# Attention scores of other groups' keys by seven products, with VectorE's order in phase 1 set by a virtual clock and convolution multiplications on GpSimd

## The chip, the cores and the metric

The kernel runs on one core of a Trainium2 chip, everything in float32. The metric is device microseconds (us) for one execution; before the change the median of three runs is 2495.1 us (2494.08 to 2495.87).

## What is computed

The input x is 4 x 2048 tokens of 512 numbers. Two blocks follow each other, each with a layer norm in front, a layer norm behind and a residual sum:

```
def _L0_attn_ref(x, Wq, bq, Wk, bk, Wv, bv, Wo, bo):
    q = relu(x @ Wq + bq); k = relu(x @ Wk + bk); v = relu(x @ Wv + bv)
    e = einsum('bqd,bkd->bqk', q, k) / sqrt(D)
    e = e - NEG * causal
    e = exp(e - max(e)); attn = e / sum(e)
    return relu(einsum('bqk,bkd->bqd', attn, v) @ Wo + bo)

def _gated_bottleneck(x2d, conv_w, conv_b, gamma, beta, lin_w, lin_b):
    xc = einsum('ngf,gf->ng', x2d.reshape(n, g, 4), conv_w) + conv_b
    xn = (xc - mean) * rsqrt(var + BN_EPS) * gamma + beta   # mean, var over all tokens
    return gelu(xn) @ lin_w.T + lin_b

x = x + _layernorm(_L0_attn_ref(_layernorm(x), ...))
x = x + _layernorm(_L0_ffn_ref(_layernorm(x), ...))   # two branches gated by the top 32 of a softmax
```

The batch norm's mean and variance run over all 8192 tokens. So a phase 1 (attention, and the features xc of both branches) has to end before phase 2 (softmax, top 32, products with the weight) can begin. For scores that could not be masked by -10000 alone there is a second path with every key; it isn't executed with these inputs.

## The kernel before

**Tiling.** Phase 1 goes through 16 groups of 512 tokens, four of each batch (`n.g` is 0 to 3 in the batch). A group attends to its own keys, under the causal mask, and to those of the batch's earlier groups. So its scores have `n.nk` = 4 (g+1) tiles of 128 keys by 512 queries. They are kept transposed (keys on partitions) in the pool `stp` of 16 tiles.

**Seven products.** Projections with Wv, Wq, Wk and Wo (`Seven`, L390 on) are Strassen products in Winograd's form: halves of 256 in each of the three dimensions, seven products in place of eight. One product is `times` (L403): 4 matmuls of 128x128 weights by 256 columns. p1, p6, p7 and p4 add up in one PSUM accumulator, which is read out between them (`put`, L426): VectorE adds the copied sums b, c5 and c53 (products 2, 5 and 5+3, copied by ScalarE, L423) to the accumulator, so each of these products waits for the sum before it. The right operands are sums of quarters of the tokens (`token_sums`, L366), the left ones sums of weights that are made once, stored to HBM and fetched for each group through a `Ring` of 14 tiles of 256 KB (L267 on). For Wo the left operand is made of the values (`value_sums`, L376).

**One step** (`steps`, L687 on) works on group n and prepares the next one, nxt. PE's order is written down by hand (`manual_schedule(engines={PE})`, L846):

1. `scores` (L489): for each tile of keys 4 matmuls (L499), a copy by ScalarE (L508), mask (L511) and maximum (L518) on VectorE. `between` puts the group's seven products with Wo (object O), the next group's transposed tokens and their sums in between.
2. V of nxt, the fold of the maxima (L527, L529), Q of nxt, `spread` of the maxima by a matmul (L542), K of nxt.
3. `weights` (L544): subtraction on VectorE (L550), exponential on ScalarE (L551), sums on GpSimd (L555).
4. `attend` (L567) for four tiles of 128 queries, then `attended` (L581) evicts it, `residual` (L585 on) does two layer norms with the reciprocal square root on GpSimd (L137) and the residual sum x1 on GpSimd (L593), and `convolve` multiplies with both branches' weights (L613) and reduces by four (L614), all on VectorE. Then come DMAs of x1, xn2, its transpose and the transposed features.

The tile scheduler orders VectorE, ScalarE, GpSimd and SP's queue in these steps: by priority, among what is ready by its own model of time. All loads and stores named above go through SP's queue in one order.

**The end of phase 1.** In the last step the products of `bound` (L652, four pieces, `filler`) stand in for the missing projections: one after the scores, one after the fold, two after the first features of the last group. `prepare` (L661 on) readies the branches in groups 1 and 2: its second half, from L670 on, transposes the linear weights and makes three rows of bfloat16 parts with a single buffer (`prep`), each sent off by a DMA before the next is made.

Of the kernel before, what the change touches and what calls it, by code (L numbers as in the profile page):

```python
# [26 lines left out]
F32 = mybir.dt.float32  # L28
# [24 lines left out]
def sandwich_kernel(ctx: ExitStack, tc: tile.TileContext, io: dict, out: bass.AP):  # L53
# [75 lines left out]

    xn2_d = [dram.tile([GT, D], F32, name=f"xn2_{i}") for i in range(NGRP)]  # L130
# [65 lines left out]
    def phase1(every_key):  # L196
# [5 lines left out]
        kp = enter("kp", GB)  # L202
# [3 lines left out]
        ap = enter("ap", 3)  # L206
# [10 lines left out]
        def load(b, g, joint=True):  # L217

            n = Group()
            n.b, n.g, n.i = b, g, b * GB + g  # L220
            n.x = []
            n.rstd = sm.tile([P, TPG], F32, name="rstd_x")
            var = sm.tile([P, TPG], F32, name="var_x")
            n.mv = sm.tile([P, TPG, nc.vector.BN_AGGR_DIM], F32, name="mv_x")
            for t in range(TPG):
                xt = xp.tile([P, D], F32, name="xt")
                row = n.i * GT + t * P
                nc.sync.dma_start(xt, xf[row : row + P, :])
                st = sm.tile([P, nc.vector.BN_STATS_DIM], F32, name="st_x")
                nc.vector.bn_stats(st, xt)  # L230
                nc.vector.bn_aggr(n.mv[:, t, :], st)
                n.x.append(xt)
                if not joint:
                    nc.vector.tensor_scalar_add(var[:, t : t + 1], n.mv[:, t, 1:2], LN_EPS)
                    inv_sqrt(n.rstd[:, t : t + 1], var[:, t : t + 1])
            if joint:
                nc.vector.tensor_scalar_add(var, n.mv[:, :, 1], LN_EPS)
                inv_sqrt(n.rstd, var)
            return n
# [12 lines left out]
        def turn_x(n):  # L252

            for t in range(TPG):
# [5 lines left out]
                nc.sync.dma_start(xnT_d[n.i][t * P : (t + 1) * P, :], n.x[t])  # L260

# [5 lines left out]
        class Ring:  # L267
# [6 lines left out]
            def fill(self):  # L274
                while len(self.made) < len(self.order):
# [4 lines left out]
                    t = wring.tile([P, D], F32, name="wb")  # L280
                    w = io[f"L0_attn_W{m}"]
# [84 lines left out]
        def token_sums(n):  # L366
# [3 lines left out]
            nc.vector.tensor_tensor(T1, B12, B11, ALU.subtract)  # L370
            nc.vector.tensor_tensor(T2, B22, T1, ALU.subtract)
            nc.vector.tensor_tensor(B12, B22, B12, ALU.subtract)
            nc.gpsimd.tensor_tensor(T4, B21, T2, ALU.subtract)
            n.right = {1: B11, 2: B21, 3: B22, 4: T4, 5: T1, 6: T2, 7: B12}

        def value_sums(n, most):  # L376
# [3 lines left out]
            if most:  # L380
                S1, S2 = (one.tile([P, 2, H], F32, name=f"T{k}") for k in (1, 2))
                nc.vector.tensor_tensor(S1, A21, A22, ALU.add)
                nc.vector.tensor_tensor(S2, S1, A11, ALU.subtract)
                nc.vector.tensor_tensor(A21, A11, A21, ALU.subtract)
                n.left = {1: A11, 2: A12, 4: A22, 5: S1, 6: S2, 7: A21}
            else:
                n.left[3] = one.tile([P, 2, H], F32, name="T4")
                nc.vector.tensor_tensor(n.left[3], A12, n.left[6], ALU.subtract)

        class Seven:  # L390


            def __init__(self, n, m):
                self.n, self.m, self.bias = n, m, biases.get(m)
                self.room = None
                if m == "o":
# [6 lines left out]
            def times(self, ps, k, new):  # L403

                i, w = self.w[(AS_RIGHT if self.m == "o" else AS_LEFT)[k]]
                w = w.rearrange("p (c d) -> p c d", c=2)
                left, right = (self.n.left[k], w) if self.m == "o" else (w, self.n.right[k])
# [10 lines left out]
                ring.drop(i)  # L418

            def copied(self, ps, pool_tag):  # L420
                t = self.room.pop() if self.room else two.tile([P, D], F32, name=pool_tag)
# [4 lines left out]
            def put(self, r, s, other=None):  # L426

                at = self.dst[:, 2 * r : 2 * r + 2, s * H : (s + 1) * H]
                acc = self.acc.rearrange("p (d t) -> p d t", d=2)
                with tc.high_priority():  # L430
                    if other is not None:
                        nc.vector.tensor_tensor(at, acc, other.rearrange("p (d t) -> p d t", d=2), ALU.add)  # L432
# [27 lines left out]
            def p6(self):  # L460
                self.times(self.acc, 6, False)
                self.put(0, 1, self.c53)

            def p7(self):
                self.times(self.acc, 7, False)
                self.put(1, 1, self.c5)

            def p4(self):
                self.times(self.acc, 4, False)
# [19 lines left out]
        def scores(n, kTs, between=None):  # L489

            n.nk = GB * TPG if every_key else (n.g + 1) * TPG
            n.st = []
            n.mx = one.tile([P, GT], F32, name="mxsum")
            for kt in range(n.nk):
                off = first(n, kt)
                ps = ps_mm.tile([P, GT], F32, name="mm")
                k = kt % TPG * P
                for c in range(NC):
                    nc.tensor.matmul(  # L499
                        ps[:, off:],  # L500
                        lhsT=kTs[kt // TPG][:, c, k : k + P],
                        rhs=n.qT[:, c, off:],
                        start=(c == 0),
                        stop=(c == NC - 1),
                    )
                st = stp.tile([P, GT], F32, name="st")
                own = kt - n.g * TPG
                nc.scalar.copy(st[:, off:], ps[:, off:])  # L508
                if 0 <= own < TPG:
                    q = slice(own * P, (own + 1) * P)  # L510
                    nc.vector.tensor_tensor(st[:, q], st[:, q], causal, ALU.add)  # L511
                if every_key and own > 0:
                    q = slice(0, min(own, TPG) * P)
                    nc.vector.tensor_scalar_add(st[:, q], st[:, q], neg_raw)
                if kt == 0:
                    nc.vector.tensor_copy(n.mx, st)
                else:
                    nc.vector.tensor_tensor(n.mx[:, off:], n.mx[:, off:], st[:, off:], ALU.max)  # L518
                n.st.append(st)
                if between:  # L520
                    between(kt)

        def fold(src, op):

            tp = ps_tp.tile([P, NC, P], F32, name="tp")
            for t in range(TPG):
                nc.tensor.transpose(tp[:, t, :], src[:, t * P : (t + 1) * P], ident)  # L527
            r = sm.tile([P, TPG], F32, name="fold")
# [3 lines left out]
        def maxima(n):  # L532

            m = fold(n.mx, ALU.max)
# [9 lines left out]
        def weights(n):  # L544

            n.sum = one.tile([P, GT], F32, name="mxsum")
            for kt in range(n.nk):
# [6 lines left out]
                else:  # L554
                    nc.gpsimd.tensor_tensor(n.sum[:, off:], n.sum[:, off:], w, ALU.add)  # L555

        def sums(n):
            s = fold(n.sum, ALU.add)
            n.rsum = sm.tile([P, TPG], F32, name="rsum")
            nc.vector.reciprocal(n.rsum, s)  # L560
# [15 lines left out]
        def attended(n, t, acc):  # L576


            a = (ap if n.nk == GB * TPG else stp).tile([P, D], F32, name="a" if n.nk == GB * TPG else "st")
# [3 lines left out]
            return a  # L583

        def residual(n, t, a):  # L585

            ti = n.i * TPG + t
            xr = two.tile([P, D], F32, name="xr")
            nc.sync.dma_start(xr, xf[ti * P : (ti + 1) * P, :])
            m, r = row_norm(sm, a, "a")  # L590
            nc.vector.tensor_scalar(a, a, m, r, ALU.subtract, ALU.mult)
# [3 lines left out]
            store = nc.scalar if n.i == NGRP - 1 else nc.sync  # L595
            store.dma_start(x1_d[n.i][t * P : (t + 1) * P, :], x1)
            m, r = row_norm(sm, x1, "x1")
            xn2 = ap.tile([P, D], F32, name="a")
# [546 lines left out]
```

## Time and profile before

| | us |
|---|---|
| median of three runs | 2495.1 |
| the profiled execution | 2491.96 |
| its span, first to last instruction | 2490.1 |
| first group's preparation (from the start) | about 130 |
| steps of groups 1 to 15, up to the last scores | 130 to 1715 |
| end of phase 1 | 1715 to 1790.3 |
| phase 2 | 1790.3 to 2490.1 |
| a batch's four steps (933.92, 1001.38, 1096.15, 1219.09 to 1368.79) | 67.5, 94.8, 122.9, 149.7 |

The page lists busy times by engine: PE (TensorE's matmuls), PEld (its weight loads, beside them), DVE (VectorE), ACT (ScalarE), POOL (GpSimd), and SP, whose queue issues DMAs. A float32 matmul appears as two instructions. Matmuls overlap, so the duration of one (592 ns for 512 columns) is longer than the distance to the next. A row of a group reads: line, engine, operation, what it writes and reads, shapes, count, busy us, mean ns of one, idle time of the engine before it and what ended that.

The costliest groups of phase 1 by busy time are the attention products L567 (424.5 us up to 1716), the scores L499 (481.6) and the seven products L410 (790.1, the sum of its rows). The granted clock is 1.00 through the steps.

### The profile page before, as it was taken

What the parts mean: (1) busy time and instruction counts of PE and PEld (TensorE: products, weight loads), DVE (VectorE), ACT (ScalarE), POOL (GpSimd) and SP (SyncE); (2) the same over time, 40 slices, a digit from 0 to 9 for tenths busy, and PEclk for the clock granted to TensorE, in tenths of its full rate; (3) what the DMA queues carried; (4) which work ended last, traced back from release to release, by engine and by line L of the source; (5) the groups of instructions that cost most, each with busy time, mean ns of one, the idle gap of its engine ahead of it and who ended that gap; (6) DMA issues with size and microseconds to landing.
All of it is one profiled execution on the core that took longest, in us unless ns stands there. A gap on an engine that the chain in (4) does not pass through costs nothing.

```text
span 2490.1 us, 27105 instructions
## 1 busy us (share of the span) xinstructions
PE 2434.8 (98%) x7778; PEld 1401.1 (56%) x7778; DVE 1715.0 (69%) x3707; ACT 1020.5 (41%) x2208; POOL 969.2 (39%) x913
## 2 busy tenths in 40 slices
PE   8999999999999999999999999999999999999997
PEld 3775756587675658767565876754333333333332
DVE  3677564567655456765645676453699999999997
ACT  2332313232231323223131332312278787878785
POOL 1122210311221031122103122212288888898986
PEclk9999999999999999999999999999999999999998
DMA  6565543466554246655434665320434444444441
GB/s 214 183 170 170 155 124 100 112 184 169 173 153 126 96 114 184 169 175 151 127 98 112 185 170 161 108 89 3 128 76 106 110 111 118 108 119 105 118 104 53
DMA packets 551902, 325.96 MB, mean 131 GB/s; under 512 B 388672, under 2 KB 443456, under 8 KB 551744
## 3 DMA queue, kind: packets, MB, share of 16 engines
q1 hardware_dynamic: 548208, 320.97, 46.3%
q10 hardware_dynamic: 3024, 2.11, 0.3%
q8 instruction: 65, 1.06, 0.2%
q0 software_dynamic: 512, 1.06, 0.1%
q14 instruction: 93, 0.76, 0.1%
HBM read 231.22 MB, written 92.80 MB: 130 GB/s over the span
## 4 chain that ended last, share of the span: by engine, by line
PE 58%; POOL 4%; ACT 4%; DVE 3%; issue 3%; DMA 1%; SPq 0%; POOLq 0%; ACTq 0%; DVEq 0%
PE mm L499 13%; PE mm L971 12%; PE acc L567 11%; PE acc L410 9%; PE mm L410 7%; PE lg L929 3%; PE tp L1038 1%; PE lg L932 1%; POOL e_si L959 1%; POOL xs L965 1%; POOL h L1078 1%; ACT L909 1%; DVE st L550 1%; POOL mxsum L555 1%; DMA xt<-in_L_attn_x_dram 1%
## 5 line engine op out<-in xcount | busy, mean ns | idle before, releaser
L499 PE MATMUL mm<-qT,kT 128*128 128x512 f32 (+3 forms) x1280 | 481.6, 529 | 0.4 <-ACT st L508 0.4
L567 PE MATMUL acc<-vo,st 128*128 128x512 f32 x1088 | 474.7, 592 | 1.4 <-ACT st L551 1.4
L499 PEld LDWEIGHTS mm<-qT,kT 128*128 128x128 f32 x1280 | 235.2, 190 | 216.5 <-issue 193.5
L567 PEld LDWEIGHTS acc<-vo,st 128*128 128x128 f32 x1088 | 205.4, 190 | 241.5 <-issue 235.2
L971 PE MATMUL mm<-w_L_ffn_weight,xnT 128*128 128x512 f32 x512 | 248.9, 609 | 0.6 <-ACT xc_si L632 0.6
L508 ACT COPY st<-mm 128x512 f32<-128x512 f32 (+3 forms) x160 | 83.2, 520 | 401.1 <-PE mm L499 400.7
L971 PE MATMUL mm<-w_L_ffn_weight,xsT 128*128 128x512 f32 x512 | 239.9, 612 | 2.6 <-ACT xsT L1044 2.6
L553 POOL COPY mxsum<-st 128x512 f32<-128x512 f32 x16 | 9.7, 609 | 543.6 <-ACT st L551 463.4
L137 POOL TENSOR_TENSOR rs_a<-ve_a,neg_half 128x1 f32<-128x1 f32 x64 | 35.4, 554 | 362.6 <-DVE ve_a L146 358.8
L518 DVE TENSOR_TENSOR mxsum<-mxsum,st 128x512 f32<-128x512 f32 (+2 forms) x144 | 95.7, 664 | 116.3 <-ACT st L508 113.9
L410 PE MATMUL acc<-T,wb 128*128 128x256 f32 x720 | 170.7, 380 | 2.8 <-DVE qT L432 2.8
L555 POOL TENSOR_TENSOR mxsum<-mxsum,st 128x512 f32<-128x512 f32 (+2 forms) x144 | 167.7, 1165 | 13.7 <-ACT st L551 2.9
L410 PE MATMUL mm<-xnT,wb 128*128 128x256 f32 x720 | 170.1, 379 | 0.0
L410 PE MATMUL acc<-xnT,wb 128*128 128x256 f32 x720 | 165.2, 379 | 0.0
L971 PEld LDWEIGHTS mm<-w_L_ffn_weight,xsT 128*128 128x128 f32 x512 | 93.1, 192 | 111.1 <-issue 94.2
L410 PEld LDWEIGHTS acc<-T,wb 128*128 128x128 f32 x720 | 135.9, 190 | 30.4 <-issue 6.5
L971 PEld LDWEIGHTS mm<-w_L_ffn_weight,xnT 128*128 128x128 f32 x512 | 92.3, 190 | 106.6 <-issue 105.5
L410 PEld LDWEIGHTS acc<-xnT,wb 128*128 128x128 f32 x720 | 136.8, 190 | 25.0 <-issue 4.5
L410 PEld LDWEIGHTS mm<-xnT,wb 128*128 128x128 f32 x720 | 135.0, 190 | 23.8 <-issue 7.2
L582 ACT ACTIVATE st<-st 128x512 f32<-128x512 f32 x48 | 30.2, 630 | 246.7 <-DVE st L581 246.7
L937 DVE MAX8 m_si<-rest_si 128x8 f32<-128x512 f32 x192 | 131.1, 683 | 0.0
L945 DVE MATCH_REPLACE8 rest_so<-m_so,rest_so 128x512 f32<-128x512 f32 x192 | 129.7, 675 | 0.0
(223 smaller groups left out, 4285.5 us busy)
## 6 DMA issues: line engine op xcount, KB each, us to landing
x<-x SPq DMA_DIRECT2D x124, 256.0 KB, 2.9
xt<-in_L_attn_x_dram SPq DMA_DIRECT2D x64, 256.0 KB, 4.5
xr<-in_L_attn_x_dram SPq DMA_DIRECT2D x64, 256.0 KB, 2.9
xn<-xn SPq DMA_DIRECT2D x64, 256.0 KB, 2.9
out_dram<-h SPq DMA_DIRECT2D x64, 256.0 KB, 2.0
wb<-Z_v SPq DMA_DIRECT2D x60, 256.0 KB, 2.8
wb<-Z_q SPq DMA_DIRECT2D x60, 256.0 KB, 3.4
wb<-Z_k SPq DMA_DIRECT2D x60, 256.0 KB, 2.6
```

Of the source, the lines that this page charges most:

```text
L137: nc.gpsimd.tensor_tensor(dst, src, neg_half[:, : src.shape[1]], ALU.pow)
L410: nc.tensor.matmul(ps[:, d * H : (d + 1) * H], lhsT=left[:, c, d * P : (d + 1) * P], rhs=right[:, c, :], start=(new and c + d == 0), stop= ...
L499: nc.tensor.matmul(ps[:, off:], lhsT=kTs[kt // TPG][:, c, k : k + P], rhs=n.qT[:, c, off:], start=(c == 0), stop=(c == NC - 1),)
L508: nc.scalar.copy(st[:, off:], ps[:, off:])
L518: nc.vector.tensor_tensor(n.mx[:, off:], n.mx[:, off:], st[:, off:], ALU.max)
L555: nc.gpsimd.tensor_tensor(n.sum[:, off:], n.sum[:, off:], w, ALU.add)
L567: nc.tensor.matmul(acc, lhsT=n.st[kt][:, t * P : (t + 1) * P], rhs=vos[kt // TPG][:, kt % TPG, :], start=(kt == 0), stop=(kt == nk - 1),)
L582: nc.scalar.activation(a, a, AF.Relu)
L929: nc.tensor.matmul(n.lg[br], lhsT=xa[n.k][br][:, n.t * P : (n.t + 1) * P], rhs=lin_T[br], start=True, stop=False)
L937: nc.vector.max(n.m8[br], n.rest[br] if k else n.lg[br])
L945: nc.vector.match_replace(n.rest[br], n.m8[br], n.rest[br], -LOWEST)
L971: nc.tensor.matmul(ps, lhsT=lhsT[:, c, :], rhs=wf[:, c, :], start=(c == 0), stop=(c == NC - 1))
```

## The change

- Scores of other groups' keys become `Seven` objects, named by the number of the keys' group. Their left operands are the keys' quarters and sums (`key_sums`, new), stored to HBM as seven tiles per group and fetched through the ring; the right ones are sums of the queries (`query_sums`, `last_query_sum`, new). The result is four `st` tiles. The sums out of PSUM are made in two pieces of 128x256, and the maxima are taken tile by tile (`maximum`). The pool of keys shrinks to one buffer.
- Scores of the group's own keys stay tile by tile (`score_tile`).
- VectorE joins PE in the order by hand. A class `Pace` keeps a virtual time of PE (advanced by `pace.pe` at each matmul group) and one of VectorE; VectorE's work comes as jobs of three ranks, generators that yield their duration and a pause. `run` emits the next piece of the first job that is ready by this clock; `flush` emits the rest of a job at once.
- `residual` and `convolve` become one generator, `chain`, of lowest rank, with at most two open at once, carried over into the next step. Its two multiplications are GpSimd's, but in the last group.
- The second half of `prepare` comes before the attention products, and in the last step three pieces of `bound` come before `spread` and one behind the features.

```
 class Pace:
+    def add(self, rank, pieces, after=0.3):
+        job = [self.t + after, pieces]
+        self.ranks[rank].append(job)
+        return job
+    def step(self, job):
+        try:
+            us, pause = next(job[1])
+            self.v = max(self.v, job[0]) + us
+            job[0] = self.v + pause
+        except StopIteration:
+            ...
+    def open(self):
+        return [*self.ranks[0], *self.ranks[1], *self.ranks[2][:2]]
+    def run(self):
+        while self.v < self.t:
+            ready = [j for j in self.open() if j[0] <= self.v]
+            if ready:
+                self.step(ready[0])
+            else:
+                self.v = min([self.t] + [j[0] for j in self.open()])
+    def pe(self, us):
+        self.t += us
+        self.run()
```

```
+        def key_sums(n):
+            A11, A21, A12, A22 = quarters(n.kT)
+            S1, S2, S4 = (one.tile([P, 2, H], F32, name=f"Q{k}") for k in (1, 2, 4))
+            nc.vector.tensor_tensor(S1, A21, A22, ALU.add)
+            ...
+            nc.vector.tensor_tensor(S4, A12, S2, ALU.subtract)
+            for k, t in ((2, A12), (5, S1), (1, A11), (3, S4), (6, S2), (7, A21), (4, A22)):
+                nc.sync.dma_start(keys_d[n.i, k].rearrange("p (c d) -> p c d", c=2), t)
+            yield 0.9, 0.0
```

The products, now with `pace.pe(1.72)` behind each, and their sums:

```
             def put(self, r, s, other=None):
+                scores = isinstance(self.m, int)
+                if other is not None:
+                    self.job = pace.add(0, work(0.8 if scores else 0.7, self.written, r, s, other))
+                else:
+                    self.written(r, s)
+                if scores and r != s:
+                    after = 0.3 if other is not None else 1.2
+                    self.n.maxima += [pace.add(1, work(0.66, self.maximum, st), after) for st in self.dst[2 * r : 2 * r + 2]]
...
             def p6(self):
+                pace.flush(self.job)
                 self.times(self.acc, 6, False)
                 self.put(0, 1, self.c53)
```

The step:

```
+                for t in range(TPG):
+                    score_tile(n, n.g * TPG + t, n.kT)
+                    pace.pe(0.86 * (TPG - t))
+                    for step in of_O[t]:
+                        step()
+                        ...
+                if n.g:
+                    pace.add(0, work(0.9, last_query_sum, n))
+                    A = Seven(n, n.b * GB)
+                    A.p2(), A.p5(), O.p7(), A.p1(), A.p3(), O.p4(), A.p6()
+                    for i in range(1, n.g):
+                        N = Seven(n, n.b * GB + i)
+                        N.p2(), N.p5(), A.p7(), N.p1(), N.p3(), A.p4(), N.p6()
+                        A = N
...
                     V = Seven(nxt, "v")
-                    V.p2(), V.p5()
+                    V.p2()
+                    pace.flush(tokens)
+                    if n.g:
+                        A.p7()
+                    V.p5()
+                    if n.g:
+                        A.p4()
```

The chain of a tile of queries:

```
+            m, r = row_norm(sm, a, "a")
+            yield 1.0, 1.1
             nc.vector.tensor_scalar(a, a, m, r, ALU.subtract, ALU.mult)
             nc.gpsimd.tensor_tensor(x1, a, xr, ALU.add)
+            yield 0.55, 1.8
             m, r = row_norm(sm, x1, "x1")
+            yield 1.0, 1.1
             nc.vector.tensor_scalar(xn2, x1, m, r, ALU.subtract, ALU.mult)
+            yield 0.55, 0.0
+            engine = nc.vector if final else nc.gpsimd
+            for br in branches:
+                pr = prp.tile([P, D], F32, name="pr")
+                engine.tensor_tensor(pr, xn2, conv_w[br], ALU.mult)
-                pr = two.tile([P, D], F32, name="x1")
-                nc.vector.scalar_tensor_tensor(pr, xn2, 1.0, conv_w[br], ALU.mult, ALU.mult)
...
-            with tc.manual_schedule(engines={PE}):
+            with tc.manual_schedule(engines={PE, mybir.EngineType.DVE}):
                 steps(n, ahead)
```

## The prediction

> **What bounds the kernel now.** I read the page first, then PE's busy time by stretch, then the chain that ended last for PE's pace, then who waits for whom.
>
> ```profile
> PE 2434.8 (98%) x7778; PEld 1401.1 (56%) x7778; DVE 1715.0 (69%) x3707; ACT 1020.5 (41%) x2208; POOL 969.2 (39%) x913
> 130.00:1715.00 1585.00, 1581.43 (x5530) 1029.51 (x5529) 949.70 (x1854) 432.37 (x876) 329.65 (x343) 1.00 0.49 140
> 1715.00:1790.30 75.30, 68.83 (x181) 31.34 (x179) 37.64 (x80) 18.25 (x42) 28.60 (x28) 0.99 0.32 90
> 1790.30:2490.10 699.80, 664.15 (x1674) 266.88 (x1674) 662.90 (x1626) 532.84 (x1218) 590.89 (x507) 0.98 0.42 103
> ```
>
> The three stretches (window, length, busy of PE, PEld, DVE, ACT, POOL, granted clock, DMA share, GB/s) are the steps of phase 1, their end, and phase 2. In the steps PE idles 3.6 us of 1585; VectorE is busy 60%, GpSimd 21%. The diff leaves phase 2 alone, so only the first two stretches can move, and in the first only less work on PE helps: there is almost no wait to win back. PE's busy time overlaps (ends of matmuls are modelled), so its pace is read from the chain of waits, where each piece follows the one before it:
>
> ```profile
> 674.32 6.87 PE mm L499 x16
> 708.87 3.46 PE mm L410 x16
> 823.29 22.36 PE mm L499 x64
> ```
>
> L499 is a score product, 6.87/16 = 0.429 us per 512-wide instruction (a float32 matmul is two). L410 is one of the seven products, 3.46/16 = 0.216 us per 256-wide one, that is 8 x 0.216 = 1.73 us per product.
>
> **The change, part by part.** *Scores.* A block of 512 queries by another group's 512 keys costs 4 tiles x 4 matmuls x 2 = 32 instructions now: 32 x 0.429 = 13.74 us. By seven products it is 7 x 1.73 = 12.10 us. Gain 1.64 us. A batch has 1+2+3 = 6 such blocks, 4 batches 24: **-39.4 us** on PE, all of it on the path, since PE is the bound there. The own group's tiles stay. This is the firm term: 256-wide products already run by the thousand in this trace at this pace.
>
> *What the blocks cost elsewhere.* VectorE: three sums per block out of PSUM, each in two pieces of 128x256; the nearest row (a 128x256 subtraction with one operand in PSUM) is 410 ns, so 24 x 6 x 0.41 = 59 us. Sums of keys, 12 groups x 4: nearest rows are those of the values, 786 to 1094 ns, mean 0.88: 42 us. Sums of queries, 12 x 3 at 0.71 (the rows of the tokens' sums): 25 us. Maxima and masks keep their number. Removed: two multiplications for 60 of the 64 tiles, 0.651 + 0.687 = 1.34 us, 80 us. Net +46 us: (950 + 46)/1545 = 64% busy. ScalarE trades four 512-wide copies (4 x 0.584) for three and two 256-wide (0.372): +0.16 us a block. GpSimd gains 60 x 2 x 1.268 (the row of its 128x512 sum x) = 152 us and 12 x 1.48 for T4, so 500 us, 32%. All of this lies under PE by volume; the tightest step is a batch's first group. There, 933.9 to 1001.4, VectorE is busy 44 of 67.5 us, and the four tiles of that group's chain go over into the next step, which has 27 us more of PE.
>
> ```profile
> 933.92:1001.38 67.46, 67.46 (x288) 53.05 (x287) 44.03 (x89) 23.72 (x49) 12.05 (x14) 1.00 0.63 182
> L384 DVE TENSOR_TENSOR vT<-vT 128x512 f32<-128x512 f32 x15 | 16.0, 1067 | 0.3
> L432 DVE TENSOR_TENSOR vo<-acc,st 128x512 f32<-128x512 f32 x45 | 30.8, 684 | 6.0 <-PE acc L410 5.9
> L593 POOL TENSOR_TENSOR x<-st,xr 128x512 f32<-128x512 f32 x48 | 60.9, 1268 | 88.2 <-issue 28.7 <-DVE st L591 24.7 <-DVE xg L614 19.3
> SPq L284 <- PE acc L410: 159.7, 92, 8.2
> ```
>
> *DMAs.* 12 x 7 stores and 24 x 7 loads of 256 KB through SP's queue: 66 MB over 1545 us, +43 GB/s on 140. Stretches at 182 to 198 GB/s run now without PE idling. At about 0.38 us of SP each it is 96 us in 1545. The stores make SP wait for VectorE, with the weights' ring, the residuals and the turned tiles queued behind; the ring's 14 tiles cover 14 x 1.73 = 24 us, while the longest present wait of the ring is 8.2 us (last row above). I cost it at nothing; with the cover gone, each store wait beyond it would be PE's, one for each of 12 groups.
>
> *VectorE's order.* It becomes fixed, emitted by a clock that assumes 1.72 us a product and 0.86 us per 512-wide matmul; the trace has 1.73 and 2 x 0.429, so it doesn't drift. What it does not know is GpSimd's queue and contention. Between the product that fills an accumulator and the next one that adds to it lie two others, 3.45 us (one, 1.73, for V's first). The hand-over needs some 0.25 us to start, 0.84 us for two pieces and 0.1 back: slack about 2.2 us. A chain step on VectorE waits for GpSimd three times a tile (rs_a, x, rs_x), and each can now stand behind the neighbour tile's two multiplications, 2.54 us; VectorE then stands at the head of its fixed order with a sum for PE behind it. Bounds: nothing (all late by less than the slack; 3.6 us of present idle may even go), and the whole pair passed on for each of 60 tiles, 152 us. Nearest is the present behaviour: VectorE waits 61 us for x (L593) and 32 for rs_x in these steps and PE loses 3.6. I take some 0.35 us past the slack, on a third of the tiles' 60 chains, plus as much again from two-input sums that lose the port: 60 x 0.33 x 0.35 = 7 us, of which 1 would be there anyway, plus 2 for bn_stats that now stand 6 us after their fetch: **+8 us**.
>
> The contention itself is in the rows: value sum L384, both operands in SBUF, averages 1067 ns where L432 with one in PSUM takes 684, and one maximum (810.24) took 1.61 us beside a GpSimd sum of 1.26 us begun at 810.04. The Trainium skill speaks against this change here ("SBUF — State Buffer", Who interferes with whom): a VectorE instruction with two SBUF inputs contends with a GpSimd instruction that reads SBUF. By that rule the moved multiplications are not free for VectorE: about 28 two-input instructions a step x 16 x 11% more of GpSimd's time x 0.6 us would be an estimated 30 us of VectorE; without it, none. Either way this is VectorE's time, and reaches PE only past the slack.
>
> *Branch preparation (L670 to L682)* moves ahead of the attention products, with its casts now in VectorE's fixed order. The row's buffer is single, so cast 2 and 3 each wait for the DMA of the row before: issue 245.50, next cast 248.31, 2.8 us, of which 1.1 us is covered by its own two instructions. That blocks VectorE 3 x 0.41 + 2 x 1.07 + 2 x 1.7 = 6.8 us in groups 1 and 2, with K's sum behind it that product K.p7 needs after the first attention tile (5 x 0.858 = 4.3 us in group 1, 7.7 in group 2). Bounds 0 and 2 x 6.8; I take 6.8 + 0.7 - 4.3 - 0.6 (transposes and fold): **+2.5 us**.
>
> *The last step.* The filler products of the bound (8 x 0.43 = 3.44 us each) were two before the spread of the maxima and two behind the attention, under the wait for VectorE's last tile (1775.6 to 1788.7). Three now come before: **+3.4 us**. The evictions of tiles 0 to 2 are emitted after attention 2, so the chains of 0 and 1 no longer run under it; four chains of 6.4 us follow from about 1763, ending near 1789.5 where they ended at 1788.5: **+1 us** (bounds -2, +5).
>
> **Sum.** -39.4 + 8 + 2.5 + 3.4 + 1 = -24.5 us. The profiled execution took 1.9 us more than its span (2491.96 against 2490.1) and 3.1 us less than the median of 2495.1; the difference is carried to the median: **2470.6 us**, 1.0% faster.
>
> **Rivals.**
> A. *PE takes the saving undisturbed*: hand-overs stay within the slack, the preparation hides: -39.4 + 3.4 + 1 - 1 = 2459 us. For it: PE lost 3.6 us although VectorE waited some 90 us for GpSimd. Against: the order is now fixed, and GpSimd's queue is half as full again. Chance 0.25.
> B. *Forecast*, waits of 8 to 25 us: 2464 to 2483. Chance 0.50.
> C. *Waits eat most of it*: 1.5 us per step more than forecast, 16 x 1.5 = 24 us, 2494 us; what is late is V's first sum (slack 0.5 us) and the token sums in a batch's first group. Chance 0.15.
> D. *Slower: GpSimd becomes VectorE's late partner.* Place: a chain's rs and x behind the neighbour's multiplications. It decides from (24.5 + 8)/60 = 0.54 us of PE waiting per tile; at 1.0 us it is 60 - 32.5 = 27 us above, 2522 us. Against: two thirds of GpSimd's time remain free, and a chain has two whole steps. Chance 0.08.
> E. *The change doesn't do what it says*: the products don't interleave, for a PSUM buffer or an st tile still held by the chain of the group before; 24 x 1.64 us would go, 2510 us. Chance 0.02.
>
> **How the numbers follow.** A measurement of this kernel can tell about 0.2%, 5 us, from none. Faster takes A, B and 0.07 of C: 0.82; same 0.07 of C; slower D, E and the last 0.01 of C: 0.11. The range runs from just under A to C's middle: 2457 to 2490; alone, the forecast's is 2464 to 2483.
>
> **What would show it.** PE's instructions fall in L499's place by 24 x 32 = 768 and rise by 24 x 56 = 1344 of 0.216 us. A group's steps should take about 67.5, 93, 119.5, 145 us (now 67.5, 94.8, 122.9, 149.7). PE's idle time before the seven products of scores, by releaser VectorE, should be 5 to 20 us in all; near zero speaks for A, above 30 for C or D, and VectorE's waits for GpSimd's rs and x tell D from C. Phase 2 must keep its 700 us. Wrong are the numbers if products of scores run slower than 1.73 us with no wait shown, or if SP's waits for the key sums exceed 20 us.

## The result, and the profile after

The changed kernel takes 2512.1 us (median of four runs, 2510.8 to 2516.5) against 2494.6 for the one before on the same chip: a ratio of 1.0073 (95% interval 1.0056 to 1.0091). The forecast was 2470.6 us, 1.0% faster, with a range up to 2490. It was wrong in sign. The profiled execution took 2513.1 us, its span is 2511.3, 21.2 us more than before.

The page's line of busy times, and the three stretches of the prediction in the kernel after (window, length, busy of PE, PEld, DVE, ACT, POOL, granted clock, DMA share, GB/s):

```profile
PE 2417.3 (96%) x8354; PEld 1520.5 (61%) x8354; DVE 1777.8 (71%) x3815; ACT 1026.5 (41%) x2232; POOL 1141.6 (45%) x1045
130.00:1736.00 1606.00, 1569.58 (x6137) 1152.48 (x6136) 1024.31 (x1994) 439.35 (x905) 506.90 (x481) 0.99 0.64 180
1736.00:1811.40 75.40, 68.16 (x168) 30.84 (x167) 40.10 (x79) 17.68 (x38) 28.34 (x28) 0.95 0.31 84
1811.40:2511.30 699.90, 665.04 (x1675) 266.84 (x1675) 663.39 (x1626) 533.84 (x1222) 591.93 (x507) 0.98 0.42 103
```

Phase 2 and the end of phase 1 are what they were (699.8 and 75.3 us before). All of the loss is in the steps, 21 us longer though PE has less to do in them: 36 us of the stretch now have no busy PE, where it was 3.6. PE fell from 98% to 96%, VectorE stands at 64%, GpSimd at 32%. No engine has become the bound by its volume.

A batch's four steps after, with the same columns:

```profile
506.48:573.94 67.46, 67.46 (x288) 53.05 (x286) 38.96 (x77) 23.74 (x49) 11.75 (x12) 1.00 0.59 176
573.94:677.81 103.87, 97.46 (x375) 71.79 (x374) 79.22 (x155) 27.97 (x58) 41.57 (x41) 0.97 0.75 215
677.81:800.70 122.89, 120.89 (x463) 87.62 (x462) 76.14 (x151) 32.62 (x67) 38.61 (x38) 0.99 0.66 179
800.70:945.46 144.76, 144.76 (x551) 103.13 (x550) 83.55 (x159) 36.87 (x76) 46.44 (x42) 1.00 0.59 163
```

Before, they were 67.5, 94.8, 122.9 and 149.7 in the batch that the prediction reads, the third (this one, the second, took 67.5, 94.8, 123.9 and 150.2); 67.5, 93, 119.5 and 145 were expected. The fourth step has what was forecast, 144.76, which is 4.94 us less than 149.70 for three blocks, 1.65 each. The second is 9 us longer than before and 11 over its forecast, and its clock is 0.97: it lost time in two ways. Both can be taken from the starts of PE's instructions, from the first scores to the last attention. Where PE waited, what lies between two starts beyond the pace (0.429 us per 512-wide instruction, 0.2155 per 256-wide one) counts as idle; where it did not wait, as running below its pace:

```
                                   before    after
PE idle in the steps, us              6.5     48.2
PE running below its pace, us         1.7     16.5
```

Balance of the span: -39.4 for the products and +3.4 for the filler (both as forecast), +41.7 idle, +14.8 below pace: +20.5, where +21.2 was measured.

Who PE waits for in the steps (engine, line, releaser: total, times, longest):

```profile
PE acc L542 <- DVE vo L594: 17.3, 10, 2.1
PE acc L542 <- DVE vT L594: 13.4, 4, 3.8
PE tp L167 <- DVE xn L319: 5.8, 3, 2.0
PE acc L542 <- DVE st L590: 3.1, 3, 1.1
```

These are the hand-overs of the prediction: products waiting for VectorE's sum `put` into the same accumulator. Before, the largest such row was this one:

```profile
PE acc L410 <- DVE qT L432: 2.8, 6, 1.1
```

Two sums stand out, O's and V's, in the second and third steps of a batch. The row `xn` is another matter, three waits in the first step of all (65.2 us instead of 57.0), where normalized tokens stand behind the mask of the own tile in VectorE's order.

The timeline around one wait for O's sum, second step of that batch (start, length, engine, line, operation; in brackets idle time before it and its releaser):

```profile
588.39 1.26 POOL L789 TENSOR_TENSOR pr<-a,convw_so 128x512 f32<-128x512 f32 x1
588.53 1.27 DVE L680 TENSOR_TENSOR st<-st,causal 128x128 f32<-128x128 f32 x1
589.48 1.89 PE L542 MATMUL acc<-wb,T 128*128 128x256 f32 x8
589.62 1.32 POOL L789 TENSOR_TENSOR pr<-a,convw_si 128x512 f32<-128x512 f32 x1
589.84 1.38 DVE L688 TENSOR_TENSOR mxsum<-mxsum,st 128x256 f32<-128x256 f32 x1
...
593.50 0.28 DVE L680 TENSOR_TENSOR st<-st,causal 128x128 f32<-128x128 f32 x1
593.66 1.27 POOL L789 TENSOR_TENSOR pr<-a,convw_so 128x512 f32<-128x512 f32 x1 [2.72 <-DVE xg L797]
593.82 1.26 DVE L688 TENSOR_TENSOR mxsum<-mxsum,st 128x128 f32<-128x128 f32 x1
596.08 0.65 DVE L594 TENSOR_TENSOR vo<-acc,st 128x512 f32<-128x512 f32 x1
596.78 2.77 PE L542 MATMUL acc<-wb,vT 128*128 128x256 f32 x8 [1.96 <-DVE vo L594]
```

Product p6 of O ends at 591.37, its sum starts only at 596.08, and PE stands 1.96 us. In front of it in VectorE's fixed order are a mask that takes 1.27 us beside a multiplication of GpSimd (0.28 at 593.50 with none beside it) and two maxima of 1.38 and 1.26 us. GpSimd's L789 runs beside each of the three, and each ends 0.15 to 0.28 us after the multiplication beside it.

The same for V's sum, some 20 us later:

```profile
610.81 1.27 POOL L789 TENSOR_TENSOR pr<-a,convw_so 128x512 f32<-128x512 f32 x1 [2.12 <-DVE a L781]
612.04 1.27 POOL L789 TENSOR_TENSOR pr<-a,convw_si 128x512 f32<-128x512 f32 x1
613.27 1.27 POOL L773 TENSOR_TENSOR x<-st,xr 128x512 f32<-128x512 f32 x1
614.58 0.70 DVE L145 BATCH_NORM_STATS2 st_x<-x 128x6 f32<-128x512 f32 x1 [2.46 <-POOL x L773]
...
616.97 1.26 POOL L789 TENSOR_TENSOR pr<-a,convw_so 128x512 f32<-128x512 f32 x1 [0.66 <-DVE a L781]
617.40 3.05 DVE L577 TENSOR_TENSOR mxsum<-mxsum,st 128x512 f32<-128x512 f32 x2
618.19 1.71 POOL L789 TENSOR_TENSOR pr<-a,convw_si 128x512 f32<-128x512 f32 x1
620.37 0.68 DVE L594 TENSOR_TENSOR vT<-acc,x 128x512 f32<-128x512 f32 x1
621.10 3.19 PE L542 MATMUL acc<-T,wb 128*128 128x256 f32 x8 [3.20 <-DVE vT L594]
```

Here two things add up. VectorE waits 2.46 us for the sum x, which stands behind the neighbour tile's two multiplications in GpSimd's queue. Then two maxima take 3.05 us beside the next pair of multiplications; the two at 608.87, with no multiplication until 610.81, took 1.41 together. The sum that PE needs stands behind both.

Groups of VectorE in the steps after (line, engine, operation, shapes, count | busy, mean ns | idle before, releaser):

```profile
L680 DVE TENSOR_TENSOR st<-st,causal 128x128 f32<-128x128 f32 x64 | 31.1, 486 | 57.2 <-ACT st L668 56.9
L688 DVE TENSOR_TENSOR mxsum<-mxsum,st 128x128 f32<-128x128 f32 x16 | 12.3, 771 | 0.6
L688 DVE TENSOR_TENSOR mxsum<-mxsum,st 128x256 f32<-128x256 f32 x16 | 10.6, 661 | 0.6
```

and the same mask before:

```profile
L511 DVE TENSOR_TENSOR st<-st,causal 128x128 f32<-128x128 f32 x64 | 18.5, 289 | 61.0 <-ACT st L508 60.8
```

The mask reads two operands from SBUF; it went from 289 to 486 ns on average, with nothing changed in it.

### The profile page after: what moved, and what is told of

Same layout as the page of the kernel before. It is cut to its first block, busy times and chain, and to the rows that moved or that the text cites. A ratio compares the mean times of both kernels' runs of the same rounds, so it can differ in the third digit from the quotient of the medians.

```text
span 2511.3 us, 29224 instructions
## 1 busy us (share of the span) xinstructions
PE 2417.3 (96%) x8354; PEld 1520.5 (61%) x8354; DVE 1777.8 (71%) x3815; ACT 1026.5 (41%) x2232; POOL 1141.6 (45%) x1045
## 2 busy tenths in 40 slices
DMA packets 594347, 392.18 MB, mean 156 GB/s; under 512 B 392705, under 2 KB 459777, under 8 KB 594177
## 4 chain that ended last, share of the span: by engine, by line
PE 80%; DVE 6%; POOL 5%; ACT 4%; issue 4%; DMA 1%; SPq 1%; POOLq 0%; ACTq 0%; DVEq 0%
PE acc L542 20%; PE acc L743 19%; PE mm L542 14%; PE mm L1198 13%; PE mm L660 5%; PE lg L1156 3%; PE mm L397 2%; PE tp L1265 2%; PE lg L1159 1%; POOL e_si L1186 1%; POOL xs L1192 1%; POOL h L1305 1%; ACT L1136 1%; DVE xg L797 1%; POOL x L773 1%
## 5 line engine op out<-in xcount | busy, mean ns | idle before, releaser
L140 POOL TENSOR_TENSOR rstd_x<-var_x,neg_half 128x4 f32<-128x4 f32 (+1 forms) x19 | 17.9, 943 | 424.6 <-DVE var_x L305 419.7
L730 POOL TENSOR_TENSOR mxsum<-mxsum,st 128x512 f32<-128x512 f32 (+2 forms) x144 | 161.5, 1121 | 13.8 <-ACT st L726 2.9
L660 PE MATMUL mm<-qT,kT 128*128 128x128 f32 (+3 forms) x512 | 150.2, 437 | 0.0
L561 ACT COPY cp<-mm 128x512 f32<-128x512 f32 x72 | 42.2, 586 | 236.6 <-PE mm L542 236.6
L1172 DVE MATCH_REPLACE8 rest_si<-m_si,rest_si 128x512 f32<-128x512 f32 x192 | 129.8, 676 | 0.0
L1164 DVE MAX8 m_so<-rest_so 128x8 f32<-128x512 f32 x192 | 129.8, 676 | 0.0
L590 DVE TENSOR_TENSOR st<-acc,cp 128x256 f32<-128x256 f32 x144 | 54.1, 417 | 102.0 <-PE acc L542 97.9
```

The lines of the kernel that those rows point to most:

```text
L140: nc.gpsimd.tensor_tensor(dst, src, neg_half[:, : src.shape[1]], ALU.pow)
L590: nc.vector.tensor_tensor(st[:, cols], acc[:, d, :], other[:, d, :], ALU.add)
L660: nc.tensor.matmul(ps[:, off:], lhsT=kT[:, c, k : k + P], rhs=n.qT[:, c, off:], start=(c == 0), stop=(c == NC - 1),)
L1164: nc.vector.max(n.m8[br], n.rest[br] if k else n.lg[br])
L1172: nc.vector.match_replace(n.rest[br], n.m8[br], n.rest[br], -LOWEST)
```

## The experiments

What had to be told apart: whether the loss came from the multiplications on GpSimd, from VectorE's fixed order, or from both together; and, of the multiplications, whether through GpSimd's queue (a chain's partner is late) or through what they read beside VectorE. In the table, idle and below pace are PE's, in one profile each, as above (e2's profile is of the slowest of its nine runs, 6 us over the median). All ratios are to the kernel before on the same chip.

```
                                     median us   ratio (95%)               idle   below pace
after                                  2512.1    1.0073 (1.0056, 1.0091)   48.2   16.5
c0  own pool for xr, x1                2524.1    1.0117 (1.0100, 1.0134)   54.5   17.8
e1  c0, multiplications on VectorE     2477.3    0.9927 (0.9911, 0.9944)   25.3    3.1
e2  c0, scheduler orders VectorE       2486.6    0.9965 (0.9955, 0.9975)   35.4   11.1
e5  e1 and e2 together                 2476.0    0.9913 (0.9890, 0.9936)   25.2    9.0
e4  c0, GpSimd writes only             2487.8    0.9966 (0.9952, 0.9981)   31.7    6.6
e4b e4, as long as the original        2488.5    0.9975 (0.9963, 0.9986)   33.8    5.4
e6  c0, one chain open                 2561.6    1.0264 (1.0244, 1.0283)   79.5   22.5
h1  after, waits filled with products  2506.1    1.0044 (1.0031, 1.0057)   28.8    4.8
b1  e1, reordered                      2467.3    0.9886 (0.9868, 0.9905)   14.6    2.0
b1g b1, multiplications on GpSimd      2504.5    1.0048 (1.0032, 1.0063)   40.9   11.5
b2  b1, preparation later              2476.1    0.9924 (0.9910, 0.9938)   20.5    5.1
```

**c0, the base of the others.** The chain's tiles xr and x1 get a pool of their own, so that the place of the multiplications can be changed alone:

```
+        chp = enter("chp", 2)
-            xr = two.tile([P, D], F32, name="xr")
+            xr = chp.tile([P, D], F32, name="xr")
-            x1 = two.tile([P, D], F32, name="x1")
+            x1 = chp.tile([P, D], F32, name="x1")
```

> The changed kernel, but the chain's residual xr and sum x1 get a pool of their own (2 buffers each) in place of the one that they share with the copies of V's, Q's and K's products. It is the reference for the next three. Theory L (GpSimd's multiplications make VectorE late, by the shared port and by standing ahead of x and rs in GpSimd's queue): nothing of that is touched, so 2505 to 2515 us and steps of a batch's second group of 101 to 104 us. Rival B (chains are late because they wait for a buffer): below 2495 us.

It is slower than the changed kernel by 12 us, which no theory had expected. Of the 8.7 us between the two profiles, 6.2 are in the second steps (102.5 to 105.9 us), and the traces show where: PE's waits for Q's sum (qT) are 7.5 us, against 2.4 in the changed kernel. One of them, in the second batch's second step:

```profile
645.11 0.69 DVE L277 BATCH_NORM_STATS2 bn_all<-xc_so 128x6 f32<-128x512 f32 x1 [1.88 <-DMA xc_so<-xgT]
647.20 0.69 DVE L277 BATCH_NORM_STATS2 bn_all<-xc_si 128x6 f32<-128x512 f32 x1 [1.39 <-DMA xc_si<-xgT]
647.81 0.67 DVE L595 TENSOR_TENSOR qT<-acc,xr 128x512 f32<-128x512 f32 x1
```

Two batch-norm instructions stand ahead of the sum in VectorE's order, and each waits until the features of the group before are fetched; VectorE waits 11.9 us there in all, against 6.5 in the changed kernel. Why the fetch lands later was not tried. What follows from e1 to e6 is measured against c0.

**e1, the multiplications back on VectorE**, with the order still fixed:

```
-            engine = nc.vector if final else nc.gpsimd
+            engine = nc.vector
-                yield 1.4 if final else 0.7, 0.0 if final else 1.0
+                yield 1.4 if final else 2.1, 0.0
```

> As the kernel with the pool of its own, but the convolutions' two multiplications are VectorE's again in all groups (its clock is told 1.4 us more for them). Theory L: the waits of PE fall to a third although VectorE has 80 us more to do; second groups' steps 94 to 97 us, total 2470 to 2485 us. Rival V (the fixed order of VectorE, or its volume in the second group's step, makes the waits): 80 us more of work make it worse, 2515 to 2540 us.

47 us less than c0. The second step of the same batch:

```profile
566.00:661.98 95.98, 93.82 (x375) 69.62 (x374) 80.42 (x165) 27.85 (x58) 27.05 (x29) 1.00 0.82 234
```

7.9 us shorter than after, at a clock of 1.00. GpSimd gives up 14.5 us of work in it, and VectorE, which takes up some ten multiplications, is busy 80.4 us against 79.2: the same work that it did without them had been that much longer. PE's waits for VectorE's sums in the steps of e1:

```profile
PE acc L543 <- DVE vT L595: 5.8, 4, 1.6
PE acc L543 <- DVE vo L595: 3.7, 7, 0.8
```

30.7 us of the two rows have become 9.5.

**e2, VectorE's order left to the scheduler**, the multiplications still on GpSimd:

```
-            with tc.manual_schedule(engines={PE, mybir.EngineType.DVE}):
+            with tc.manual_schedule(engines={PE}):
```

> As the kernel with the pool of its own, but only PE's order is by hand; VectorE's is again the tile scheduler's, multiplications stay on GpSimd. Theory L: the same collisions with GpSimd, within 12 us of 2510. Rival V: the waits go, 2465 to 2485 us; the first step's three waits of 2.2 us for transposed tokens go under both.

37 us less than c0: just above the 2465 to 2485 us that were expected if the order alone made the waits, and 11 us under the 2498 that the other theory needed. So the multiplications on GpSimd by themselves don't make the loss either.

**e5, both undone**, so that the products of scores stand almost alone.

> The kernel with multiplications on VectorE (2477.3 us), and VectorE's order again by the tile scheduler: the seven products for scores alone. Theory L+F (GpSimd's multiplications do harm because a fixed order can't step around them): with neither, the waits that are left are those of the scheduler's order, 2470 to 2485 us, within 10 us of 2477. Rival V (the fixed order itself helps the products, as it was meant to): 2490 us or more.

With e1 and c0 this makes a square. Under the fixed order the place of the multiplications is worth 47 us, under the scheduler's order 11. With GpSimd's multiplications the fixed order costs 37 us, with VectorE's about nothing (1.3 us, within the intervals). The loss is neither edit's own; it is the two together.

**e4 and e4b, GpSimd writes without reading.** The two multiplications of each tile are left out and become fills of the same tiles, so the features are computed from ones: two fills for each multiplication in e4; in e4b three and two, 5 x 0.53 = 2.7 us for the 2.54 us of the multiplications:

```
-                engine.tensor_tensor(pr, xn2, conv_w[br], ALU.mult)
+                for _ in range(3 if br == "so" else 2): engine.memset(pr, 1.0)
```

> As the kernel with the pool of its own, but each multiplication on GpSimd is replaced by two fills of its result, so GpSimd only writes; the features are then computed from ones (that part of the result is left out). GpSimd stays occupied in the same place, but reads nothing. If the shared port is the larger part of theory L: two-input sums of VectorE take 0.68 us beside GpSimd again and the total falls to 2475 to 2490 us. If its queue is the larger part: 2500 us or more, in proportion to the fills' length.

> As the run that only writes (2487.8 us), but with 3 fills for the first multiplication and 2 for the second, 5 x 0.53 = 2.7 us, so that GpSimd's queue is occupied at least as long as by the two multiplications (2.6 us); the convolutions' multiplications are left out. If the port (GpSimd's reads) is the larger part: 2485 to 2497 us. If the shorter occupation was what helped: 2505 us or more.

Both take 36 us off c0, and the length of the fills makes no difference. So time on GpSimd's queue is not what costs most, but something that the fills lack: the reads, as the durations below show. Groups of VectorE and GpSimd in e4b:

```profile
L681 DVE TENSOR_TENSOR st<-st,causal 128x128 f32<-128x128 f32 x64 | 21.8, 340 | 61.8 <-ACT st L669 61.4
L689 DVE TENSOR_TENSOR mxsum<-mxsum,st 128x128 f32<-128x128 f32 x16 | 4.7, 292 | 0.6
L794 POOL MEMSET pr<- 128x512 f32 x295 | 151.9, 532 | 136.5 <-DVE xg L802 125.6 <-DVE st L872 2.5
```

The mask is back from 486 to 340 ns and the small maximum from 771 to 292, although GpSimd spends 152 us on the fills. One place of its timeline shows it:

```profile
583.72 2.74 POOL L794 MEMSET pr<- 128x512 f32 x5 [3.27 <-DVE xg L802]
583.89 0.29 DVE L689 TENSOR_TENSOR mxsum<-mxsum,st 128x128 f32<-128x128 f32 x1
```

A maximum right beside a fill takes 0.29 us; beside a multiplication it took 1.26. The mask and the maxima are as long in c0 as in the changed kernel (482 ns for the mask, 770 for the small maximum). This is what the Trainium skill says ("SBUF — State Buffer", Who interferes with whom): VectorE with two inputs from SBUF contends with a GpSimd instruction that reads SBUF, not with one that only writes. The rows here agree. One more thing sets the fills apart: they need no input, so they start as soon as their tile is free, and not behind the normalized tokens; what share of the 36 us that is worth was not tried. Of the 11 us that still lie between e4b and e1, 8.5 are PE's waits for Q's sum, which e1 does not have, behind the same two fetches as in c0: VectorE waits 12.8 us for them in e4b and 3.4 in e1.

**e6, one chain open at a time**, so that no chain stands behind a neighbour's multiplications:

```
-                return [*self.ranks[0], *self.ranks[1], *self.ranks[2][:2]]
+                return [*self.ranks[0], *self.ranks[1], *self.ranks[2][:1]]
```

> The kernel with the pool of its own (2524.1 us, multiplications on GpSimd, fixed order), but with one chain open at a time instead of two, so that no tile's multiplications stand ahead of its neighbour's x and rs in GpSimd's queue. If the queue is the larger part: 2490 to 2500 us. If the port is: 2510 us or more, second groups' steps still above 100 us.

38 us slower than c0, and it says nothing of the queue: the chains that didn't get their turn are flushed in a lump ahead of K's products, and PE waits some 7.6 us there for Q's sum in each batch's second step, 30.5 in all. The edit brought in a larger cost than the one that it was to take away.

**h1, unused products put in front of the waits.** To the changed kernel itself, products of 0.86 us whose result nobody reads are added where PE would wait, two before O.p7 and three before V.p6 in the second step, two before O.p6 in the third: 28 x 0.86 = 24 us of more work for PE.

```
+            def busy(k):
+                tp = ps_tp.tile([P, NC, P], F32, name="tp")
+                for _ in range(k):
+                    nc.tensor.matmul(tp..., lhsT=ident, rhs=bo, start=True, stop=True)
...
+                    if n.g == 1:
+                        busy(2)
```

> The changed kernel (2512.1 us) with unused products of PE in place of its longest waits: 2 x 0.86 us ahead of O.p7 in second groups, 2 x 0.86 us ahead of O.p6 in third groups, 3 x 0.86 us ahead of V.p6 in second groups; 28 products of 0.86 us, 24 us of PE's time. Theory H (after a wait of about 2 us and more PE runs at half its pace for some 4 us, which costs 1.9 us each time): the waits are filled, the half pace goes, 2495 to 2504 us although PE does more. Rival: the half pace is not the wait's doing, or more work just adds: 2511 us or more.

24 us more work, 6 us less time (the intervals of the two ratios just touch). In the profiles the idle time falls by 19.4 us and the time below pace by 11.7: 24 - 19.4 - 11.7 = -7. So the lost pace follows the waits and is a cost of its own. The expected 2495 to 2504 was missed by 2 us; 28.8 us of idle time are left.

**b1, another order by hand**, with the multiplications on VectorE. In the first step of all the normalized tokens come ahead of the mask; between any two products of one accumulator stand two others, for V and Q too:

```
-                    V.p1(), V.p3(), V.p6()
...
-                    Q.p2(), Q.p5(), V.p7(), Q.p1(), V.p4()
+                    L = A if n.g else O
+                    L.p7()
+                    V.p1(), V.p3()
+                    L.p4()
+                    V.p6()
+                    Q = Seven(nxt, "q")
+                    Q.p2(), Q.p5()
...
+                    V.p7(), Q.p1(), V.p4()
```

> The kernel with multiplications on VectorE (2477.3 us), and three edits to the order: the first step's normalized tokens are emitted ahead of the mask of the own tile (8 us of waits there); V's, A's and O's products interleave so that two products lie between those of one accumulator, with Q.p2 and Q.p5 ahead of the fold (1.4 to 1.8 us in four steps); sums of the weights are folded after the first attention product in second groups too (1 us in three steps). Theory: the waits left in the steps are slack between products, 2477 - 8 - 6 - 4 - 4 = 2455 us, up to 2462. Rival: VectorE's volume holds the steps, 2468 us or more, only the first step's part is gained.

The fastest kernel here, 1.1% under the one before and 45 us under the changed one. The same second step:

```profile
558.92:652.39 93.47, 93.36 (x375) 69.72 (x374) 79.99 (x161) 27.90 (x58) 27.36 (x29) 1.00 0.81 236
```

It has the 93 us that the prediction gave a second step, and the first step is back at 57.2 us. The expected 2455 to 2462 was missed by 5: the second step in which the branches are prepared takes 96.9 us where the other three take 93.1 to 94.1, and the first step of each later batch is 1 us longer than before.

**b1g, that order with GpSimd's multiplications.**

> The reordered kernel (2467.3 us) with the multiplications on GpSimd again. If two products of slack are enough for what GpSimd makes late: within 8 us of 2467. Theory L: lateness is above that slack in second groups, 2490 to 2505 us.

37 us more than b1, as theory L had it. PE's waits in its steps:

```profile
PE acc L550 <- DVE vo L602: 22.5, 12, 3.5
PE acc L550 <- POOL rs_x L140: 6.5, 4, 2.2
```

V's sums are as little late as in b1 (2.6 us in all), but O's, 3.5 us in b1, are late by 22.5. Two products between, 3.45 us, are not slack enough. The second row is put down to GpSimd's rs_x, but what these products need is a sum of scores by VectorE: in the second batch it ends at 608.68, PE starts at 608.78, and VectorE had waited 3.08 us for x ahead of it. That part is GpSimd's queue.

**b2, the preparation of the branches back behind the attention**, in b1.

> The reordered kernel (2467.3 us) with the second half of prepare behind the attention products again, as before the change. Its casts wait on VectorE for the DMAs of single rows ahead of K's sums; steps 1 and 2 took 3.4 and 0.8 us more than their like: 2463 us. If those are first-time costs of another kind, no change within 1 us.

9 us slower than b1, where 4 less were expected. The second step gains 2.9 us, the third and fourth of the first batch lose 4.1 and 5.6. In this order, the place that the change gave the preparation was the better one.

## Why the prediction was wrong

**The products of scores: right.** -39.4 us was 24 x 1.64; the steps with no waits show 1.65 a block, and nothing of it was lost to DMAs: 66.2 MB more (392.18 against 325.96), and PE waits for no fetched tile of them.

**Volumes: right, and no help.** GpSimd's 500 us in the steps are 506.9. VectorE's 950 + 46 = 996 us are 1024.3. The difference, 28 us, has the size of the estimate of 30 us that the prediction worked out from the skill's page as VectorE's loss at the port; the mask and the maxima alone are 24.5 us longer than in e1. It was named, and in PE's term it was to cost "as much again" as the late chains; but 60 x 0.33 x 0.35 = 6.9 holds no second share. With it the term would have been some 15 us, still a quarter of what was paid.

**The hand-overs, +8 us: this term failed.** Idle time and lost pace together are 41.7 + 14.8 = 56.5 us. The sentence that failed is "Either way this is VectorE's time, and reaches PE only past the slack", together with the slack of 2.2 us that it leans on. The slack was that of a sum that VectorE starts on at once. In a fixed order the sum inherits the delay of everything in front of it: at 588.5 to 595.1 three instructions lose together (1.27 - 0.28) + (1.38 - 0.48) + (1.26 - 0.29) = 2.9 us, more than the slack (the 0.48 and 0.29 are the means of these maxima in e1), and at 617.4 two lose 1.6 us on top of 2.46 of waiting. The nearest case that it leaned on, "the present behaviour", came from an order that the scheduler had made, and e2 and e5 show that this order would have paid 11 us where the fixed one paid 47. The waits also were not spread thinly over a third of the chains, as 60 x 0.33 x 0.35 assumed: those over 0.6 us are 24 in all, sit mostly at the same places in every batch, and take up to 4.0 us each. The 2 us for batch-norm instructions behind their fetch, part of the same term, fit: PE's waits for Q's sum are 2.4 us.

**Lost pace: not in the sum at all.** 14.8 us, a quarter of these 56.5, have no counterpart in the prediction.

**Branch preparation, +2.5 us: not seen.** The step with it takes 103.3 us, the other three second steps 102.8 on average. In b1, where less hides it, it shows (96.9 against 93.1 to 94.1).

**The last step, +3.4 and +1.** The last step shrank by 0.4 us: three blocks save 4.9, 1.2 are lost to waits, which leaves 3.3 for the filler. From the last attention to phase 2 it takes 15.2 us instead of 14.7, +0.5.

**The rivals.** D had the right price, 1.0 us a tile; (41.7 + 14.8)/60 = 0.94 was paid. But it had 8%, and the prediction looked for it in the wrong place. It was to show in VectorE's waits for rs and x; these fell, from 125 us (four rows together) to 61, with 21 more for the products pr. The largest rows before, then after (engine, what it waits with, releaser: total, times, longest):

```profile
DVE st_x L142 <- POOL x L593: 64.7, 49, 2.6
DVE a L599 <- POOL rs_x L137: 32.9, 53, 0.7
```

```profile
DVE st_x L145 <- POOL x L773: 43.5, 30, 3.1
DVE xg L797 <- POOL pr L789: 21.2, 28, 1.4
```

Time that an engine loses in longer instructions appears in no table of waits, only in the mean durations of its groups. The argument against D, that two thirds of GpSimd's time remain free, did not touch the mechanism: what counts is what runs beside GpSimd in the third that it uses. E is excluded by the fourth step, A and C by the size of the waits.

## What to carry to other kernels

Where an engine's order is fixed and another engine waits inside it, price a contention by the sum of what all instructions ahead of the awaited one can lose, not by the awaited one alone. Look for contention in the mean durations of unchanged groups, for waits don't show it. In such an order, ask also of every instruction that waits for a fetch what stands behind it. Moving work off an engine that is not the bound is worth nothing by volume, and here it cost 47 us of 2477.

## What the runs showed of the hardware

**PE's pace after a wait.** Taken from the starts of its instructions, PE has 15 waits over 2 us in the steps after. 8 of them were followed by a stretch at half pace that cost 1.4 to 1.8 us; of the 9 waits of 0.6 to 1.6 us, none was. Windows behind the two waits shown above and one at pace between them (the granted clock is the third number from the end):

```profile
596.80:601.40 4.60, 4.60 (x14) 3.76 (x15) 4.50 (x9) 0.00 (x0) 0.95 (x3) 0.63 0.42 143
601.40:606.00 4.60, 4.60 (x23) 4.06 (x22) 3.36 (x9) 0.91 (x2) 2.50 (x3) 1.00 0.28 80
621.10:624.90 3.80, 3.80 (x12) 3.11 (x13) 1.97 (x4) 0.89 (x2) 0.00 (x0) 0.59 0.36 133
```

Right after each wait PE gets through some 60% of its matmuls, at a granted clock of 0.63 and 0.59, and a few microseconds later through all. A wait of 2 us that is followed by such a stretch so costs nearly 4, and that is why 24 us of unused products made the kernel 6 us faster (h1). The Trainium skill ("TensorE: Matmul & The Clock Gate", Part 1: The HAM clock gate) has the clock halve after an idle window of some 3.4 us, one that runs freely; here waits of 2.1 to 2.2 us were enough in 5 of 11 cases, and those of 3.4 to 4.0 in 3 of 4. The clock's own record tells these cases apart. The stretch behind the first wait lasts 3.41 us at a clock of 0.50:

```profile
597.86:601.27 3.41, 3.41 (x10) 2.70 (x9) 3.31 (x8) 0.00 (x0) 0.61 (x2) 0.50 0.44 150
```

All 8 last as long, and they begin whole multiples of 3.413 us apart: the next two begin at 621.75 and 696.84, 7 and 29 such steps after 597.86. On this grid, each of the 8 waits had 2.0 us or more within the one step before the slow one. The 7 others were cut in two by a border of the grid, and their longer part was 1.1 to 2.0 us; what decided lies near 2.0 us of idle time in one step. So the same wait of 2.1 us cost 2 us or 4, by where it fell.

**What stays open.** Why the fetched features land later with an own pool for xr and x1 (c0) and with fills (e4b) than with multiplications on VectorE (e1), and how much of e4b's gain comes from fills starting earlier than multiplications can.
